# An attention stage: pixels' softmax in pieces of 128, and the norm's squares on ScalarE

## The chip, the core and the metric

The kernel runs as one launch on one core of a Trainium2 chip. The metric is the device time of that launch in microseconds (us), as the median of several runs. Engines are named as in the profile: PE is TensorE's matmul stream, PEld its weight loads, DVE is VectorE, ACT is ScalarE, POOL is GpSimd, SP is SyncE, which issues most transfers.

## The reference

Four layers follow one another on an image tensor x of 32 x 192 x 56 x 56 in float32. Each adds to x a function of its group norm (32 groups of 6 channels): agent attention, a scan over the pixels in both directions, a shift with a small blur, and a long convolution by FFT. The change lies in the first layer alone:

```python
def _gn(v, G=32, eps=1e-5):                 # mean and variance of a group: 6 channels, all pixels
    m = mean(g); s = var(g)
    return (g - m) / sqrt(s + eps)

q, k, v = split(xf @ Wqkv + bqkv)           # n = 3136 pixels, 6 heads of 32 channels
agent = q averaged over 8 x 8 pixels        # 49 agents
agent_attn = softmax(agent * scale @ k.T + pos_bias, over the pixels)
agent_v = agent_attn @ v                    # 49 values for each head
q_attn = softmax(q * scale @ agent.T + agent_bias, over the 49 agents)
out = q_attn @ agent_v + depthwise_3x3(v)
x = x + out @ proj_w + proj_b
```

`pos_bias` and `agent_bias` are sums of a 7 x 7 grid that is enlarged linearly to 56 x 56, a term for each row and a term for each column.

## The kernel before, in words

The attention stage runs from about 147 to 4985 us and goes through the 32 images one after the other. An image lies in SBUF as two tiles: channels 0 to 127 (`x[0]`, 128 x 3136), and channels 128 to 191 with the upper half of the rows on partitions 0 to 63 and the lower half on 64 to 127 (`x[1]`, 128 x 1568). The columns are cut into four chunks of 16, 16, 16 and 8 (`WIDTHS`). A wide chunk holds 896 pixels, the narrow one 448.

The logits of attention need no q and k of their own: `seen` (L582) multiplies the agents into the weights, which gives `gk` and `gq` (128 rows for the first channels) and `gk_c`, `gq_c`. These last hold the other 64 channels and a row of ones, and below them constant coefficients, by which the same matmul adds the bias: 28 rows for the pixel rows of one half of the image, 16 for the columns and 16 for a 4 x 4 part of the grid. There is one set of such coefficients for each chunk and half, eight in all; the first 65 rows are the same in each and are copied to all of them by one DMA for each image (L593, on SP's queue, from the tile `once`).

For one image the code does this.
- For each chunk j: `weigh(j)` (L651) makes the logits of 98 agent rows (two heads) against the pixels on TensorE, takes their maximum on VectorE (`low`, L661) and the exponential on ScalarE (`pr`, L663); `turn_v` and `turn` transpose; `gather` (L697) multiplies by v, `settle` (L711) sorts the heads; `find_v` makes v of a later chunk, `convolve` (L634) makes the depthwise convolution by eight products and sums on VectorE (L646). `moments` (L507) of the next image stands after the last chunk.
- `ask(0)`, then `join` (L721), which makes `values`. `ask(j)` (L743) is the pixels' softmax: pieces of 112 pixels on the partitions, 294 columns (6 heads of 49 agents). Two pieces share a PSUM tile; each takes a matmul over the first channels (L751) and one over the rest with the bias (L752), a maximum (L755) and a subtraction (L756) on VectorE. Four pieces share an exponential on ScalarE (L764), a sum (L766), a reciprocal and a product (L768) on VectorE.
- For t from 1 to 5: `ask(t)`; `turn_back(t-1)` (L771), in which TensorE transposes the pieces (L778) and ScalarE copies the three results to `pqT` (L782); `project(t-2)` (L799), which multiplies by the projection, adds the image and lets ScalarE take squares for the next layer's norm (L819); and `answer(t-1)` (L786), whose matmuls multiply `pqT` by `values` (L791, L796), added on VectorE (L793, L797). Between them lies the next image's preparation: `spread_of` (L545) at t = 1, `scaling` (L555) and `normed` (L596) at t = 2 and after, `find_agents` at t = 2.

The next image's group norm comes from `moments` and two small matmuls. `moments` takes mean and variance of each partition by VectorE's bn_stats over seven pieces of `x[0]` (L512) and four of `x[1]` (L514) and aggregates them (L516, L517). It also sums 8 pixels each (`by_x`, L521) for the agents' average. `grouped` (L538) averages over a group's channels with a constant matrix; `spread_of` uses it for the mean and forms the squared difference from it (`d`), `scaling` uses it for the variance.

The tile framework puts the instructions in order on each engine and inserts the waits. An engine works strictly in its own order. The PSUM pool has four tiles of two banks; the SBUF tag "weights", which `pr` and `pqT` share, has five buffers, "turned" two.

Of the kernel before, what the change touches and what calls it, by code (L numbers as in the profile page):

```python
# [20 lines left out]
F32 = mybir.dt.float32  # L21
# [385 lines left out]
class _Ready:  # L407


    def __init__(self, pool, images):  # L410
        self.images = images

        def new(name, shape):
            return pool.tile(shape, F32, name=name, tag=name)

        self.w, self.c, self.k = new("att_w", [128, 1240]), new("att_c", [65, 770]), new("att_k", [128, 704])
        self.gk_c, self.gq_c = (new(n, [128, 2 * len(WIDTHS), HA]) for n in ("gk_c", "gq_c"))
        self.xs_c = [new(f"xs_c{j}", [128, S * w]) for j, w in enumerate(WIDTHS)]

    def image(self, nc, a, b):  # L420
# [17 lines left out]
def attention(ctx: ExitStack, tc: tile.TileContext, a, ready, x1, st_a, st_c, beside):  # L438
# [16 lines left out]
    UP, LOW = slice(0, 64), slice(64, 128)  # L455
    HALVES = ((0, UP), (1, LOW))
    P2 = slice(0, PAIR)

    def psum():
        return pp.tile([128, 2, BANK], F32, name="ps", tag="ps")  # L460
# [30 lines left out]
    def small(name, shape):  # L491
        return sp.tile(shape, F32, name=name, tag=name)
# [5 lines left out]
    def sizes(j):  # L498
        w = WIDTHS[j]
        return w, 28 * w, 28 * w // SUB  # L500
# [5 lines left out]

    def moments(x):  # L507

        st_a, st_c = small("st_a", [128, 7, 6]), small("st_c", [128, 4, 6])
        flat = [t.rearrange("p y x -> p (y x)") for t in x]  # L510
        for i in range(7):
            nc.vector.bn_stats(st_a[:, i], flat[0][:, i * 448 : (i + 1) * 448])  # L512
        for i in range(4):
            nc.vector.bn_stats(st_c[:, i], flat[1][:, i * 392 : (i + 1) * 392])  # L514
        mv = small("mv", [128, 2, 2])
        nc.vector.bn_aggr(mv[:, 0], st_a.rearrange("p a b -> p (a b)"))  # L516
        nc.vector.bn_aggr(mv[:, 1], st_c.rearrange("p a b -> p (a b)"))  # L517
        pool_a, pool_c = small("pool_a", [128, AG]), small("pool_c", [65, AG])
        by_x = [wp.tile([128, n, POOL], F32, name="by_x", tag=f"by_x{n}", bufs=1) for n in (S, S // 2)]
        for t in range(2):  # L520
            nc.vector.tensor_reduce(  # L521
                by_x[t].rearrange("p y q -> p (y q)"), x[t].rearrange("p y (q x) -> p (y q) x", x=8), AX.X, ALU.add
            )
        nc.vector.tensor_reduce(
            pool_a.rearrange("p (w q) -> p w q", w=POOL), by_x[0].rearrange("p (w y) q -> p w q y", y=8), AX.X, ALU.add
        )
        fours = small("fours", [64, 2 * POOL, POOL])
        for h, r in HALVES:
            nc.vector.tensor_reduce(
                fours[:, h * POOL : (h + 1) * POOL], by_x[1][r].rearrange("p (w y) q -> p w q y", y=4), AX.X, ALU.add  # L530
            )
        nc.vector.tensor_tensor(
            pool_c[0:64].rearrange("p (w q) -> p w q", w=POOL), fours[:, 0::2], fours[:, 1::2], ALU.add
        )
        nc.vector.memset(pool_c[64:65], 1.0)
        return mv, (pool_a, pool_c)
# [5 lines left out]
                mm(ps[:, 0, t : t + 1], norm4[:, 2 * s + t], src[s], start=(s == 0), stop=(s == 1))  # L542
        return ps[:, 0, 0:2]

    def spread_of(mv):  # L545

        mean = small("mean", [128, 2])
        nc.vector.tensor_copy(mean, grouped([mv[:, t, 0:1] for t in range(2)]))
        d = small("d", [128, 2])
        nc.vector.tensor_tensor(d, mv[:, :, 0], mean, ALU.subtract)  # L550
        nc.vector.tensor_tensor(d, d, d, ALU.mult)
        nc.vector.tensor_tensor(d, d, mv[:, :, 1], ALU.add)
        return mean, d

    def scaling(mean, d, pools):  # L555
# [26 lines left out]
    def seen(ag, w, to_c, name):  # L582

        ps = psum()
        for i, cols in enumerate((slice(0, 128), slice(128, C + 1))):
            n = (128, 65)[i]
            mm(ps[:n, i, : 4 * AG], w[0][:, cols], ag[0], start=True, stop=True)
            mm(ps[:n, i, 4 * AG : HA], w[1][:, cols], ag[1], start=True, stop=True)
        g = small(name, [128, HA])
        nc.scalar.copy(g, ps[:, 0, :HA])  # L590
        c = sp.tile([65, HA], F32, name="once", tag="once", bufs=1)
        nc.scalar.copy(c, ps[0:65, 1, :HA])
        nc.sync.dma_start(out=to_c[0:65], in_=c.unsqueeze(1).to_broadcast([65, 2 * NK, HA]))  # L593
        return g

    def normed(x, rs, nb, j):  # L596
# [54 lines left out]
    def weigh(j, g, low, sums):  # L651
        _, n, _ = sizes(j)
        prs = []
        for p in range(3):
# [7 lines left out]
            pr = wp.tile([PAIR, 2, CH], F32, name="pr", tag="weights", bufs=5)  # L662
# [77 lines left out]
        return values  # L740


    def ask(j, g):  # L743
        _, _, ns = sizes(j)
        pq = wp.tile([SUB, 8, HA], F32, name="pq", tag="turned", bufs=2)
        for q0 in range(0, 2 * ns, 4):
            for q in range(q0, q0 + 4, 2):
                ps = psum()
                for i in range(2):
                    px = slice((q + i) * SUB, (q + i + 1) * SUB)  # L750
                    mm(ps[:SUB, i, :HA], xs_a[j][:, px], g, start=True, stop=False)  # L751
                    mm(ps[:SUB, i, :HA], xs_c[j][0:KC, px], gq_c[0:KC, 2 * j + (q + i) // ns], start=False, stop=True)  # L752
                by_head = ps[:SUB, :, :HA].rearrange("p i (h g) -> p i h g", g=AG)
                mx = sp.tile([SUB, 2, HEADS], F32, name="mx", tag="mx", bufs=4)
                nc.vector.tensor_reduce(mx, by_head, AX.X, ALU.max)  # L755
                nc.vector.tensor_tensor(  # L756
                    pq[:, q : q + 2].rearrange("p i (h g) -> p i h g", g=AG),
                    by_head,
                    _bc(mx, [SUB, 2, HEADS, AG]),
                    ALU.subtract,  # L760
                )
            flat = pq[:, q0 : q0 + 4].rearrange("p i c -> p (i c)")
            rows = flat.rearrange("p (r g) -> p r g", g=AG)
            nc.scalar.activation(flat, flat, AF.Exp)  # L764
            sm = sp.tile([SUB, 4 * HEADS], F32, name="sm", tag="sm", bufs=4)
            nc.vector.tensor_reduce(sm, rows, AX.X, ALU.add)  # L766
            nc.vector.reciprocal(sm, sm)
            nc.vector.tensor_tensor(rows, rows, _bc(sm, [SUB, 4 * HEADS, AG]), ALU.mult)  # L768
        return pq

    def turn_back(j, pq):  # L771
        _, n, ns = sizes(j)
        out = []
        for p in range(3):
            ps = psum()
            for q in range(2 * ns):
                h, s = divmod(q, ns)
                nc.tensor.transpose(  # L778
                    ps[P2, h, s * SUB : (s + 1) * SUB], pq[:, q, p * PAIR : (p + 1) * PAIR], ident[:SUB, :SUB]
                )  # L780
            t = wp.tile([PAIR, 2, CH], F32, name="pqT", tag="weights", bufs=5)
            nc.scalar.copy(t[:, :, :n], ps[P2, :, :n])  # L782
            out.append(t)
        return out

    def answer(j, pqT, values, o):  # L786
        _, n, _ = sizes(j)
        ps = psum()
        for h in range(2):
            for p, r in HALVES:  # L790
                mm(ps[r, h, :n], values[:, p], pqT[p][:, h, :n], start=True, stop=True)  # L791
        got = o[0].rearrange("p (h n) -> p h n", h=2)
        nc.vector.tensor_tensor(got, got, ps[:, :, :n], ALU.add)  # L793
        ps = psum()
        for h, r in HALVES:
            mm(ps[r, 0, :n], values[:, 2], pqT[2][:, h, :n], start=True, stop=True)  # L796
        nc.vector.tensor_tensor(o[1], o[1], ps[:, 0, :n], ALU.add)  # L797

    def project(j, o, x, st):  # L799
# [23 lines left out]

    nxt = ready.first
    mv, pools = moments(nxt)
    rs, nb = scaling(*spread_of(mv), pools)
    ag = find_agents(0, pools)
    gk = seen(ag, wkT, gk_c, "gk_a")
    for j in range(NK):
# [3 lines left out]
    for b in range(NB):  # L833
# [1063 lines left out]
    return np.stack([w[0:128], np.pad(w[128:C], ((0, 64), (0, 0)))], 1)  # L1897


def _coefficients(grid, cols, rows):  # L1900

    grid, cols, rows = grid.reshape(HA, POOL, POOL), cols.reshape(HA, S), rows.reshape(HA, S)
    out = np.zeros((KC - 65, 2 * len(WIDTHS), HA), grid.dtype)
    for j, w in enumerate(WIDTHS):
        for h in range(2):
            to = out[:, 2 * j + h]
            to[0:28] = rows[:, 28 * h : 28 * h + 28].T
            to[28 : 28 + w] = cols[:, STARTS[j] : STARTS[j] + w].T
            to[44:60] = grid[:, 3 * h : 3 * h + 4, GRID[j] : GRID[j] + 4].reshape(HA, 16).T
    return out  # L1910


def _laid_out(inputs):
# [22 lines left out]
    out["coef_q"] = _coefficients(a["L0_conv_na_bias"], cols, rows)  # L1936
# [41 lines left out]
```

## Time and profile before

| what | us |
|---|---|
| median of 3 runs | 10783.73 |
| lowest and highest | 10777.28, 10800.41 |
| profiled execution, its own time | 10811.08 |
| its span in the trace | 10809.3 |
| mean granted TensorE clock | 0.95 of full speed |

The page of the profile gives, for the whole span, 9604.3 us of PE (89%), 9260.0 us of DVE (86%), 6372.8 us of ACT (59%) and 2918.0 us of POOL (27%). In the attention stage POOL does nothing. The transfer that ends an image (L888) is issued 32 times, the first at 347.2 us and the last at 4983.8, so an image takes 149.6 us on average.

A row of the timeline gives start and duration in us, the engine, the line, the operation with its output and inputs, partitions x elements and type, the number of instructions put together, and in brackets the idle time before with what ended it. A row of a group gives busy time, mean ns of one, and idle time before with what ended it. A window's row is explained where it is shown.

### The profile page before, as it was taken

How to read it: one execution, taken by the hardware profiler on the slowest of the kernel's cores; microseconds unless marked ns; L12 is line 12 of the kernel's file. 1: busy time of each engine (PE TensorE's matmuls, PEld its weight loads, DVE VectorE, ACT ScalarE, POOL GpSimd, SP SyncE). 2: the span in 40 equal slices, each digit the busy share in tenths (PEclk: the TensorE clock that was granted, in tenths of full speed). 3: DMA queues.
4: the chain of work that ended last, by engine and by line, in shares of the span. 5: the costliest groups of instructions: out<-in, count | busy, mean ns of one | idle time of the engine just before them, and what ended most of it. 6: DMA issues, size and time to landing. Idle time of an engine off the chain costs nothing. (4 is left out here: it accounts for less than half of the span.)

```text
span 10809.3 us, 166766 instructions
## 1 busy us (share of the span) xinstructions
PE 9604.3 (89%) x64806; PEld 5959.0 (55%) x64806; DVE 9260.0 (86%) x11668; ACT 6372.8 (59%) x11964; POOL 2918.0 (27%) x2614
## 2 busy tenths in 40 slices
PE   6999999999999999998888888888888799999998
PEld 3555555555555555554333333333333577787876
DVE  5888888888888888887999999999999577777877
ACT  3555555555555555554666666666666466666766
POOL 0000000000000000002655555555555444444441
PEclk8999999999999999998999999999999899999999
DMA  4211221112121111111344333333444589999998
GB/s 122 63 47 49 63 64 63 37 58 63 64 63 35 61 46 46 46 34 56 92 102 98 97 97 97 97 97 97 97 101 103 153 269 273 274 275 273 278 274 264
DMA packets 1104877, 1240.31 MB, mean 115 GB/s; under 512 B 773091, under 2 KB 807200, under 8 KB 1091992
## 3 DMA queue, kind: packets, MB, share of 16 engines
q1 hardware_dynamic: 1083148, 1201.53, 38.8%
q10 hardware_dynamic: 20932, 28.02, 1.0%
q8 instruction: 516, 8.45, 0.3%
q14 instruction: 281, 2.30, 0.1%
HBM read 915.94 MB, written 306.43 MB: 113 GB/s over the span
## 5 line engine op out<-in xcount | busy, mean ns | idle before, releaser
L646 DVE SCALAR_TENSOR_TENSOR o<-v_a,att_w,o 128x896 f32<-128x896 f32 (+1 forms) x1024 | 1053.3, 1029 | 421.7 <-ACT v_a L620 296.6
L1163 POOL MEMSET f<- 128x1 f32 x96 | 8.8, 98 | 4842.7 <-DMA st_c<-st 4837.7
L1543 DVE STREAM_TRANSPOSE z<-turned 128x1792 f32<-128x1792 f32 x192 | 677.4, 3528 | 258.3 <-ACT turned L1543 257.8
L1543 ACT COPY y<-ps 64x252 f32<-64x252 f32 (+1 forms) x2304 | 784.0, 340 | 157.9 <-PE ps L1543 128.1
L1156 ACT ACTIVATE q<-q 128x784 f32<-128x784 f32 x384 | 328.3, 855 | 813.6 <-DVE q L1151 638.5
L663 ACT ACTIVATE pr<-ps,low 98x896 f32<-98x896 f32 (+1 forms) x384 | 352.3, 918 | 567.8 <-DVE low L661 567.8
L911 PE MATMUL ps<-sq,fixed 128*128 128x392 f32 x512 | 296.8, 742 | 427.7 <-ACT sq L1234 427.7
L764 ACT ACTIVATE pq<-pq 112x1176 f32<-112x1176 f32 x224 | 265.3, 1184 | 683.3 <-DVE pq L756 654.1
L751 PE MATMUL ps<-gq_a,xs_a 128*112 128x294 f32 x1792 | 609.0, 422 | 46.6 <-DVE pq L756 24.1
L1543 POOL TENSOR_TENSOR xn<-x,scale 128x896 f32<-128x896 f32 x192 | 328.4, 1711 | 1192.3 <-DMA x<-x 759.4
L646 DVE SCALAR_TENSOR_TENSOR o<-v_c,att_w,o 128x448 f32<-128x448 f32 (+1 forms) x1024 | 634.3, 619 | 7.5 <-ACT v_c L631 2.4
L659 PE MATMUL ps<-xs_a,gk_a 128*98 128x448 f32 (+1 forms) x1536 | 638.9, 497 | 0.0
L660 PE MATMUL ps<-xs_c,gk_c 125*98 125x448 f32 (+1 forms) x1536 | 631.3, 492 | 0.0
L911 PE MATMUL ps<-x,weights 128*128 128x392 f32 x1536 | 573.7, 516 | 31.1 <-DVE bv L1185 14.1
L752 PE MATMUL ps<-gq_c,xs_c 125*112 125x294 f32 x1792 | 581.4, 411 | 0.0
L1543 PEld LDWEIGHTS ps<-toep,y 128*32 128x32 f32 x16896 | 508.2, 151 | 113.4 <-ACT y L1543 109.2
L1543 PE MATMUL ps<-toep,y 128*32 128x112 f32 x16896 | 554.8, 287 | 0.0
L1543 PE MATMUL ps<-rows,xn 128*112 128x112 f32 x3072 | 378.5, 281 | 159.6 <-POOL xn L1543 136.0
L1543 ACT ACTIVATE turned<-ps,rs 128x448 f32<-128x448 f32 (+1 forms) x576 | 384.4, 668 | 203.4 <-PE ps L1543 195.7
L1543 PE MATMUL ps<-fixed,padded 128*128 128x168 f32 x3072 | 490.0, 314 | 0.0
L766 DVE TENSOR_REDUCE sm<-pq 112x24 f32<-112x1176 f32 x224 | 307.7, 1374 | 181.9 <-ACT pq L764 181.9
L1543 PEld LDWEIGHTS ps<-fixed,padded 128*128 128x128 f32 x3072 | 455.6, 195 | 2.4 <-issue 1.9
(367 smaller groups left out, 25548.6 us busy)
## 6 DMA issues: line engine op xcount, KB each, us to landing
toep<-spans SPq DMA_DIRECT2D x192, 2352.0 KB
x<-x SPq DMA_DIRECT2D x576, 392.0 KB
x<-x SPq DMA_DIRECT2D x896, 196.0 KB
out_x<-done SPq DMA_DIRECT2D x384, 196.0 KB
spans<-lags SPq DMA_DIRECT2D x24, 2352.0 KB
x<-in_x SPq DMA_DIRECT2D x32, 1568.0 KB
x<-x SPq DMA_DIRECT2D x32, 1568.0 KB
x<-in_x SPq DMA_DIRECT2D x64, 392.0 KB
```

The source lines that it names most:

```text
L646: nc.vector.scalar_tensor_tensor(dst, tap(i), dww[:, t, i : i + 1], dst, ALU.mult, ALU.add)
L659: mm(ps[P2, h, :n], g[:, cols], xs_a[j][:, px], start=True, stop=False)
L660: mm(ps[P2, h, :n], gk_c[0:KC, 2 * j + h, cols], xs_c[j][0:KC, px], start=False, stop=True)
L663: nc.scalar.activation(pr[:, :, :n], ps[P2, :, :n], AF.Exp, bias=low[:, j, p : p + 1], accum_out=sums[:, j, p : p + 1])
L751: mm(ps[:SUB, i, :HA], xs_a[j][:, px], g, start=True, stop=False)
L752: mm(ps[:SUB, i, :HA], xs_c[j][0:KC, px], gq_c[0:KC, 2 * j + (q + i) // ns], start=False, stop=True)
L764: nc.scalar.activation(flat, flat, AF.Exp)
L766: nc.vector.tensor_reduce(sm, rows, AX.X, ALU.add)
L911: mm(out, aa, srcs[t][h], start=True, stop=False)
L1156: nc.scalar.activation(den, den, AF.Ln)
L1163: nc.gpsimd.memset(s, 0.0)
L1543: return lambda *args, **kw: self.tc.keep_in_program_order(do(*args, **kw))
```

## The change: pieces of 128 pixels, and squares about the mean

For the three wide chunks, `ask` and `turn_back` use seven pieces of 128 pixels in place of eight of 112. The fourth piece lies across the two halves of the image (the last 64 pixels of one and the first 64 of the other), so it gets a set of coefficients of its own: for each wide chunk a third one, made of 14 rows of either half and of the grid rows that they need. `gq_c` grows from 8 to 11 sets. The pieces are grouped as 2 + 2 and 2 + 1. The narrow chunk keeps four pieces of 112.

The norm's second moment is no longer taken by bn_stats. `moments` sums `by_x` to one number for each partition and tile. `spread_of` makes the group's mean from it, and ScalarE then squares x about that mean in six instructions of 784 elements that sum their results; VectorE adds the parts. The squares write to a tile of the tag "weights", whose buffers are cut from five to four.

```diff
-        self.gk_c, self.gq_c = (new(n, [128, 2 * len(WIDTHS), HA]) for n in ("gk_c", "gq_c"))
+        self.gk_c, self.gq_c = (
+            new(n, [128, k, HA]) for n, k in (("gk_c", 2 * len(WIDTHS)), ("gq_c", 2 * len(WIDTHS) + 3))
+        )
...
+    WB = 4
...
     def moments(x):
-        st_a, st_c = small("st_a", [128, 7, 6]), small("st_c", [128, 4, 6])
-        flat = [t.rearrange("p y x -> p (y x)") for t in x]
-        for i in range(7):
-            nc.vector.bn_stats(st_a[:, i], flat[0][:, i * 448 : (i + 1) * 448])
-        for i in range(4):
-            nc.vector.bn_stats(st_c[:, i], flat[1][:, i * 392 : (i + 1) * 392])
-        mv = small("mv", [128, 2, 2])
-        nc.vector.bn_aggr(mv[:, 0], st_a.rearrange("p a b -> p (a b)"))
-        nc.vector.bn_aggr(mv[:, 1], st_c.rearrange("p a b -> p (a b)"))
...
         for t in range(2):
             nc.vector.tensor_reduce(
                 by_x[t].rearrange("p y q -> p (y q)"), x[t].rearrange("p y (q x) -> p (y q) x", x=8), AX.X, ALU.add
             )
+            nc.vector.tensor_reduce(mv[:, t : t + 1], by_x[t].rearrange("p y q -> p (y q)"), AX.X, ALU.add)
...
-    def spread_of(mv):
-        mean = small("mean", [128, 2])
-        nc.vector.tensor_copy(mean, grouped([mv[:, t, 0:1] for t in range(2)]))
-        d = small("d", [128, 2])
-        nc.vector.tensor_tensor(d, mv[:, :, 0], mean, ALU.subtract)
-        nc.vector.tensor_tensor(d, d, d, ALU.mult)
-        nc.vector.tensor_tensor(d, d, mv[:, :, 1], ALU.add)
+    def spread_of(x, mv):
+        for t in range(2):
+            nc.vector.tensor_scalar(mv[:, t : t + 1], mv[:, t : t + 1], 1.0 / (N // (1 + t)), None, ALU.mult)
+        mean, away = small("mean", [128, 2]), small("away", [128, 2])
+        nc.vector.tensor_copy(mean, grouped([mv[:, t : t + 1] for t in range(2)]))
+        nc.vector.tensor_scalar(away, mean, -1.0, None, ALU.mult)
+        parts, d = small("parts", [128, 6]), small("d", [128, 2])
+        for i in range(6):
+            t, y = (0, 14 * i) if i < 4 else (1, 14 * (i - 4))
+            sq = wp.tile([128, 2 * CH], F32, name="sq", tag="weights", bufs=WB)
+            nc.scalar.activation(
+                sq[:, : 14 * S], x[t][:, y : y + 14].rearrange("p y x -> p (y x)"), AF.Square, bias=away[:, t : t + 1],
+                accum_out=parts[:, i : i + 1],
+            )
+        nc.vector.tensor_reduce(d[:, 0:1], parts[:, 0:4], AX.X, ALU.add)
+        nc.vector.tensor_reduce(d[:, 1:2], parts[:, 4:6], AX.X, ALU.add)
+        for t in range(2):
+            nc.vector.tensor_scalar(d[:, t : t + 1], d[:, t : t + 1], 1.0 / (N // (1 + t)), None, ALU.mult)
         return mean, d
...
-        nc.sync.dma_start(out=to_c[0:65], in_=c.unsqueeze(1).to_broadcast([65, 2 * NK, HA]))
+        nc.sync.dma_start(out=to_c[0:65], in_=c.unsqueeze(1).to_broadcast([65, to_c.shape[1], HA]))
...
+    def pieces(j):
+        if WIDTHS[j] < 16:
+            return SUB, [2 * j + k // 2 for k in range(4)]
+        return 128, [2 * j + k // 4 if k != 3 else 2 * NK + j for k in range(7)]
+
     def ask(j, g):
-        _, _, ns = sizes(j)
-        pq = wp.tile([SUB, 8, HA], F32, name="pq", tag="turned", bufs=2)
-        for q0 in range(0, 2 * ns, 4):
-            for q in range(q0, q0 + 4, 2):
+        m, which = pieces(j)
+        n = len(which)
+        pq = wp.tile([128, n, HA], F32, name="pq", tag="turned", bufs=2)[:m]
+        for q0 in range(0, n, 4):
+            e = min(q0 + 4, n)
+            for q in range(q0, e, 2):
+                u = min(q + 2, e)
                 ps = psum()
-                for i in range(2):
-                    px = slice((q + i) * SUB, (q + i + 1) * SUB)
-                    mm(ps[:SUB, i, :HA], xs_a[j][:, px], g, start=True, stop=False)
-                    mm(ps[:SUB, i, :HA], xs_c[j][0:KC, px], gq_c[0:KC, 2 * j + (q + i) // ns], start=False, stop=True)
+                for k in range(q, u):
+                    px = slice(k * m, (k + 1) * m)
+                    mm(ps[:m, k - q, :HA], xs_a[j][:, px], g, start=True, stop=False)
+                    mm(ps[:m, k - q, :HA], xs_c[j][0:KC, px], gq_c[0:KC, which[k]], start=False, stop=True)
...
     def turn_back(j, pq):
-            for q in range(2 * ns):
-                h, s = divmod(q, ns)
-                nc.tensor.transpose(
-                    ps[P2, h, s * SUB : (s + 1) * SUB], pq[:, q, p * PAIR : (p + 1) * PAIR], ident[:SUB, :SUB]
-                )
-            t = wp.tile([PAIR, 2, CH], F32, name="pqT", tag="weights", bufs=5)
-            nc.scalar.copy(t[:, :, :n], ps[P2, :, :n])
+            ps = psum().rearrange("p a b -> p (a b)")
+            for k in range(n):
+                nc.tensor.transpose(ps[P2, k * m : (k + 1) * m], pq[:, k, p * PAIR : (p + 1) * PAIR], ident[:m, :m])
+            t = wp.tile([PAIR, 2 * CH], F32, name="pqT", tag="weights", bufs=WB)
+            nc.scalar.copy(t[:, : n * m], ps[P2, : n * m])
...
             if more and t == 1:
-                mean, d = spread_of(mv)
+                mean, d = spread_of(nxt, mv)
```

More of the change, by code (lines that the diff above doesn't have):

```diff
@@ L507, in moments @@
     def moments(x):
-        st_a, st_c = small("st_a", [128, 7, 6]), small("st_c", [128, 4, 6])
-        flat = [t.rearrange("p y x -> p (y x)") for t in x]
-        for i in range(7):
-            nc.vector.bn_stats(st_a[:, i], flat[0][:, i * 448 : (i + 1) * 448])
-        for i in range(4):
-            nc.vector.bn_stats(st_c[:, i], flat[1][:, i * 392 : (i + 1) * 392])
-        mv = small("mv", [128, 2, 2])
-        nc.vector.bn_aggr(mv[:, 0], st_a.rearrange("p a b -> p (a b)"))
-        nc.vector.bn_aggr(mv[:, 1], st_c.rearrange("p a b -> p (a b)"))
-        pool_a, pool_c = small("pool_a", [128, AG]), small("pool_c", [65, AG])
+        pool_a, pool_c, mv = small("pool_a", [128, AG]), small("pool_c", [65, AG]), small("mv", [128, 2])
         by_x = [wp.tile([128, n, POOL], F32, name="by_x", tag=f"by_x{n}", bufs=1) for n in (S, S // 2)]
@@ L661, in weigh @@
             nc.vector.tensor_reduce(low[:, j, p : p + 1], ps[P2, :, :n], AX.XY, ALU.max, negate=True)
-            pr = wp.tile([PAIR, 2, CH], F32, name="pr", tag="weights", bufs=5)
+            pr = wp.tile([PAIR, 2, CH], F32, name="pr", tag="weights", bufs=WB)
             nc.scalar.activation(
@@ L740, in join @@
         return values
+    def pieces(j):
+        if WIDTHS[j] < 16:
+            return SUB, [2 * j + k // 2 for k in range(4)]
+        return 128, [2 * j + k // 4 if k != 3 else 2 * NK + j for k in range(7)]
     def ask(j, g):
-        _, _, ns = sizes(j)
-        pq = wp.tile([SUB, 8, HA], F32, name="pq", tag="turned", bufs=2)
-        for q0 in range(0, 2 * ns, 4):
-            for q in range(q0, q0 + 4, 2):
-                ps = psum()
-                for i in range(2):
-                    px = slice((q + i) * SUB, (q + i + 1) * SUB)
[L751 to L754, printed above, removed]
+        m, which = pieces(j)
[5 more added lines that the diff above has]
+                u = min(q + 2, e)
+                ps = psum()
+                for k in range(q, u):
+                    px = slice(k * m, (k + 1) * m)
+                    mm(ps[:m, k - q, :HA], xs_a[j][:, px], g, start=True, stop=False)
+                    mm(ps[:m, k - q, :HA], xs_c[j][0:KC, px], gq_c[0:KC, which[k]], start=False, stop=True)
+                by_head = ps[:m, : u - q, :HA].rearrange("p i (h g) -> p i h g", g=AG)
+                mx = sp.tile([128, 2, HEADS], F32, name="mx", tag="mx", bufs=4)[:m, : u - q]
@@ L755, in ask @@
                 nc.vector.tensor_reduce(mx, by_head, AX.X, ALU.max)
                 nc.vector.tensor_tensor(
-                    pq[:, q : q + 2].rearrange("p i (h g) -> p i h g", g=AG),
+                    pq[:, q:u].rearrange("p i (h g) -> p i h g", g=AG),
                     by_head,
-                    _bc(mx, [SUB, 2, HEADS, AG]),
+                    _bc(mx, [m, u - q, HEADS, AG]),
                     ALU.subtract,
                 )
-            flat = pq[:, q0 : q0 + 4].rearrange("p i c -> p (i c)")
+            flat = pq[:, q0:e].rearrange("p i c -> p (i c)")
@@ L763, in ask @@
             rows = flat.rearrange("p (r g) -> p r g", g=AG)
             nc.scalar.activation(flat, flat, AF.Exp)
-            sm = sp.tile([SUB, 4 * HEADS], F32, name="sm", tag="sm", bufs=4)
+            sm = sp.tile([128, 4 * HEADS], F32, name="sm", tag="sm", bufs=4)[:m, : (e - q0) * HEADS]
             nc.vector.tensor_reduce(sm, rows, AX.X, ALU.add)
             nc.vector.reciprocal(sm, sm)
-            nc.vector.tensor_tensor(rows, rows, _bc(sm, [SUB, 4 * HEADS, AG]), ALU.mult)
+            nc.vector.tensor_tensor(rows, rows, _bc(sm, [m, (e - q0) * HEADS, AG]), ALU.mult)
@@ L769, in ask @@
         return pq
     def turn_back(j, pq):
-        _, n, ns = sizes(j)
+        m, which = pieces(j)
+        n = len(which)
         out = []
         for p in range(3):
-            ps = psum()
-            for q in range(2 * ns):
-                h, s = divmod(q, ns)
-                nc.tensor.transpose(
-                    ps[P2, h, s * SUB : (s + 1) * SUB], pq[:, q, p * PAIR : (p + 1) * PAIR], ident[:SUB, :SUB]
-                )
-            t = wp.tile([PAIR, 2, CH], F32, name="pqT", tag="weights", bufs=5)
-            nc.scalar.copy(t[:, :, :n], ps[P2, :, :n])
+            ps = psum().rearrange("p a b -> p (a b)")
[3 more added lines that the diff above has]
+            nc.scalar.copy(t[:, : n * m], ps[P2, : n * m])
@@ L790, in answer @@
             for p, r in HALVES:
-                mm(ps[r, h, :n], values[:, p], pqT[p][:, h, :n], start=True, stop=True)
+                mm(ps[r, h, :n], values[:, p], pqT[p][:, h * n : (h + 1) * n], start=True, stop=True)
         got = o[0].rearrange("p (h n) -> p h n", h=2)
@@ L795, in answer @@
         for h, r in HALVES:
-            mm(ps[r, 0, :n], values[:, 2], pqT[2][:, h, :n], start=True, stop=True)
+            mm(ps[r, 0, :n], values[:, 2], pqT[2][:, h * n : (h + 1) * n], start=True, stop=True)
         nc.vector.tensor_tensor(o[1], o[1], ps[:, 0, :n], ALU.add)
@@ L825, in attention @@
     mv, pools = moments(nxt)
-    rs, nb = scaling(*spread_of(mv), pools)
+    rs, nb = scaling(*spread_of(nxt, mv), pools)
     ag = find_agents(0, pools)
@@ L1897, in _by_rows, with _coefficients @@
     return np.stack([w[0:128], np.pad(w[128:C], ((0, 64), (0, 0)))], 1)
-def _coefficients(grid, cols, rows):
+def _coefficients(grid, cols, rows, middle=0):
     grid, cols, rows = grid.reshape(HA, POOL, POOL), cols.reshape(HA, S), rows.reshape(HA, S)
-    out = np.zeros((KC - 65, 2 * len(WIDTHS), HA), grid.dtype)
+    out = np.zeros((KC - 65, 2 * len(WIDTHS) + middle, HA), grid.dtype)
     for j, w in enumerate(WIDTHS):
@@ L1909, in _coefficients @@
             to[44:60] = grid[:, 3 * h : 3 * h + 4, GRID[j] : GRID[j] + 4].reshape(HA, 16).T
+    for j in range(middle):
+        to = out[:, 2 * len(WIDTHS) + j]
+        to[:] = out[:, 2 * j]
+        to[0:14] = out[0:14, 2 * j + 1]
+        to[44:60] = grid[:, [3, 4, 2, 3], GRID[j] : GRID[j] + 4].reshape(HA, 16).T
     return out
@@ L1935, in _laid_out @@
     rows, cols = (np.swapaxes(a[f"L0_conv_{n}_bias"].reshape(HEADS, S, AG), 1, 2) for n in ("ha", "wa"))
-    out["coef_q"] = _coefficients(a["L0_conv_na_bias"], cols, rows)
+    out["coef_q"] = _coefficients(a["L0_conv_na_bias"], cols, rows, 3)
     out["scan_w"] = np.concatenate(
```

## The prediction

> **What bounds the kernel now.** I read the page first, then a table of windows, then TensorE's waits in the attention stage (350 to 4980 us), then the timeline of one image, engine by engine.
>
> The windows (stretch, its length, then busy time and instructions of PE, PEld, DVE, ACT, POOL, then granted clock, DMA share, GB/s) show a stage that is TensorE's: 191 of 200 us, VectorE next, ScalarE with 86 us free.
> ```profile
> 2400.00:2600.00 200.00, 191.00 (x1038) 114.97 (x1038) 161.60 (x246) 113.66 (x199) 0.00 (x0) 0.97 0.15 46
> ```
> TensorE's waits there (total us, times, longest) say where the other 9 us go. The first, 3.1 us once per image, is the largest:
> ```profile
> PE ps L542 <- DVE pq L756: 70.9, 23, 3.1
> PE ps L911 <- DVE o L793: 31.7, 30, 1.1
> PE ps L778 <- ACT pqT L782: 26.0, 33, 1.0
> PE ps L751 <- DVE pq L756: 24.1, 30, 0.9
> ```
> The timeline of TensorE at that place (start, duration, line; the idle time before in brackets):
> ```profile
> 2542.04 0.66 PE L752 MATMUL ps<-gq_c,xs_c 125*112 125x294 f32 x2
> 2545.78 1.84 PE L542 MATMUL ps<-mv,att_k 128*128 128x1 f32 x8 [3.08 <-DVE pq L756]
> 2547.81 4.31 PE L778 MATMUL ps<-att_k,pq 112*98 112x112 f32 x24 [0.19 <-DVE pq L756]
> 2552.05 1.72 PE L791 MATMUL ps<-pqT,values 98*64 98x448 f32 x8
> 2553.61 0.92 PE L796 MATMUL ps<-pqT,values 98*64 98x448 f32 x4
> 2554.46 0.75 PE L751 MATMUL ps<-gq_a,xs_a 128*112 128x294 f32 x2
> 2562.50 0.95 PE L542 MATMUL ps<-d,att_k 128*128 128x1 f32 x8
> 2567.23 1.77 PE L911 MATMUL ps<-o,att_w 128*128 128x448 f32 x4 [0.23 <-ACT pqT L782]
> ```
> VectorE is the late one there: it works without a break from 2476.5 to about 2552.6, and ask(1)'s last subtraction ends at 2551.0. On ScalarE the three copies of turn_back(0) end at 2553.1, and answer(0) and ask(2) follow:
> ```profile
> 2550.27 0.76 DVE L756 TENSOR_TENSOR pq<-ps,mx 112x588 f32<-112x588 f32 x1
> 2551.16 0.10 DVE L548 COPY mean<-ps 128x2 f32<-128x2 f32 x1
> 2551.28 1.38 DVE L768 TENSOR_TENSOR pq<-pq,sm 112x1176 f32<-112x1176 f32 x1
> 2552.16 0.91 ACT L782 COPY pqT<-ps 98x896 f32<-98x896 f32 x1 [0.21 <-PE ps L778]
> ```
> From ask(2) on to the next image TensorE hardly stops. So what delays ask(2) is paid.
>
> **The clock.** The stall has a second price. Around it the granted clock falls to a half:
> ```profile
> 2541.36:2544.77 3.41, 1.34 (x6) 0.64 (x4) 3.41 (x5) 0.00 (x0) 0.00 (x0) 1.00 0.02 5
> 2544.77:2548.18 3.41, 2.21 (x10) 2.18 (x11) 3.41 (x6) 0.42 (x1) 0.00 (x0) 0.50 0.00 0
> 2548.18:2551.60 3.42, 3.42 (x21) 3.42 (x20) 3.40 (x7) 2.23 (x3) 0.00 (x0) 0.50 0.00 0
> 2551.60:2555.01 3.41, 3.41 (x19) 1.52 (x18) 1.89 (x2) 2.34 (x3) 0.00 (x0) 1.00 0.00 0
> ```
> A stretch of 3.41 us in which TensorE works 1.3 us is followed by half clock, and full clock comes back after a full stretch. The eight tiny L542 matmuls take 1.84 us there and 0.95 us at 2562.50; the 24 transposes 4.31 us. The path doesn't pay for most of this today, because VectorE is late anyway.
>
> **Part 1: pieces of 128 pixels.** A wide chunk's softmax takes 7 pieces instead of 8, so three chunks save 6 matmuls per image. L751 and L752 start 0.248 us apart per record, two records each: 0.497 us per matmul, 6 x 0.497 = 3.0 us of TensorE. The transposes L778 move the same columns: nothing. VectorE saves an eighth of 0.76, 0.76, 1.37 and 1.37 us rows: about 1.3 us per wide chunk. ScalarE's second exponential shrinks from 1176 to 882 elements, 0.3 us. The third set of coefficients makes the copy of `once` into gq_c 11 blocks instead of 8, 0.82 MB instead of 0.60, on SP's queue; it is issued in weigh(0) and first used by ask(0), some 55 us later: nothing. Without that cover it would be, at the stage's 46 GB/s, 5 us an image at most.
>
> **Part 2: the norm's sums.** VectorE loses 7 statistics at 0.53 us, 4 at 0.47 and 0.4 of aggregates: 6.0 us; it gains small reduces, scales and one negation, about 1 us. ScalarE gets six squares of 784 elements. The nearest rows are its squares in project, which start 1.03 us apart at 896 elements and 0.65 at 448, accumulator read included; so 0.94 each, 5.6 us. Bounds: 0.65 and 1.03 each, 3.9 to 6.2 us; I take 0.94, between them by size.
>
> By the Trainium skill's page ScalarE: Activation LUTs ("What ACT_TABLE_LOAD costs" has the times of an ACTIVATE) such an instruction with one pointer operand takes 280 ns + 0.833 ns per element, less 93 ns back to back; as an estimate 0.84 us each, 5.0 us for six, without an accumulator read. By it the forecast would be 0.6 us an image lower, some 19 us in all; the rows of project, which have the read, stand nearer.
>
> If all that were hidden, an image would lose 3.0 us of TensorE work and the 3.1 us stall.
>
> **Part 3: where the squares stand.** This decides. spread_of is still called at t = 1, after ask(1) and before turn_back(0). In the changed kernel's order ScalarE has: both exponentials of ask(1), six squares, the three copies pqT of turn_back(0), ask(2)'s exponential. Before, nothing of the norm was on ScalarE there. The squares need `away`, which VectorE makes from the group's mean; in its order this is behind ask(1)'s first product and second sum. So:
> - Ask(0) and ask(1) start and run quicker. The statistics no longer stand between the convolution and ask(0), but TensorE's first pair, ready at 2527.5 today, comes about 1.4 later (the gather's wait of part 4), 2528.9, where today mx starts at 2530.12; so VectorE's relief of 5 us is worth only 1.2 us; the shorter rows give 1.5. The last subtraction ends about 2548.3 instead of 2551.0.
> - Behind it come reciprocal and mean 0.3, product 1.38, sum 1.03 (three quarters of 1.37), away 0.1: 2551.2.
> - Six squares: 2556.9. Three copies, 0.81 us start to start: 2559.5, against 2553.1. Answer(0), whose matmuls wait for them, and ask(2), queued behind it on TensorE: about 2561.0 against 2554.46, **+6.5 us**.
> - Ask(2) has two matmuls less, -1.0; the 1.0 us stall before the later L778 rows and the 0.23 at L911 go, since what they wait for is long done. At project: **+4.2 us**.
> - VectorE's sums of the squares stand ahead of its addition L793 and of ask(2)'s maxima, but both wait for PE work that comes later anyway: nothing. The buffers of "weights" go from 5 to 4; each reuse waits for work that TensorE does earlier in its order: nothing, and 0.3 us if a square waits for the one before.
>
> **Part 4: the clock after it.** TensorE now idles some 10 us in that place, in two pieces around the transposes. It resumes at half clock, which lasts for the rest of the stretch it resumes in and, unless that rest is nearly whole, for one more: 3.4 to 5.1 us on average, I take 4.6, in which half the work is lost, +2.3. In the middle of convolve(2), the 3.35 us reduction by_x now stands where three statistics (1.67 us) stood, ahead of the maxima `low` that the exponentials, the turned weights and the gather of chunk 1 wait for; the gather then waits 2.1 us instead of 0.59, which may bring one more slow window: +0.8. The short slow stretch after the 1.0 us stall, in every other image, goes: -0.85. Together +2.2. Bounds of the clock's part: -0.85 (the lost slow stretch alone) and +5 (slow until two full windows). I take 2.2, as the rows above show a return after one.
>
> The Trainium skill's page TensorE: Matmul & The Clock Gate ("What's actually happening") has the clock fall after an idle window and return after a busy one. The row with 1.3 us of work in its window disagrees, since that window wasn't idle. By the page the gather's 2.1 us would cost no clock, and the sum would be 0.8 us an image, 25 us in all, lower. Its advice against gaps of over 3 us ("Why this matters for your kernels") speaks against this change.
>
> **The sum.** 4.2 + 2.2 = 6.4 us an image; 31 images have a next one: +198. The first image's norm has nothing beside it: by_x (5.1 us) and the squares (5.6) now both come before its first normed pixel, where the statistics were done at 78 us, before the matmuls that wait for other loads (147): +11 at most, which I take. The last image has neither squares nor statistics, -3. Together +206 on the profiled execution of 10811 us: 11,017. The median of the runs was 27 us lower: **10,990 us**.
>
> **The rivals.**
> - Slower without the clock: resumption at full speed, 31 x 4.2 + 8 = +138, 10,922 from the median. For: the half clock today is mostly hidden. Against: TensorE has work only for half of the windows before ask(2).
> - Slower, with more: two slow windows each image, 4.2 + 4.6 = 9 us an image, 31 x 9 + 8 = +287, 11,071.
> - **Faster**: the squares run before turn_back(0) is ready. It decides where `away` is there 6 us ahead of the first transpose's end, thus about 2543. Then each image loses 3.0 + 3.1 us: -190, 10,594; half of it, 10,690, if they fit in part. For: VectorE is relieved by 5 us before ask(0) and ScalarE is free from 2538.7 to 2547.8. Against: the order puts `away` behind ask(1)'s exponentials.
> - No change: the whole of VectorE's 7 us is had before ask(1)'s end (2544), which cancels the +6.5: within 20 us of 10,784. It fails where TensorE paces ask(0), as 2528.9 says.
>
> **How the numbers follow.** Forecast 0.50; without the clock 0.20; more clock 0.15; faster 0.11; no change 0.04. About 0.2% (22 us) is what a measurement can tell. Faster 0.11, same 0.04, slower 0.85. The range, 10,820 to 11,110, leaves out the faster cases and the top of the strongest clock.
>
> **What would show it.** L542's first matmul earlier than before, ScalarE with six squares back to back right before the three pqT copies, TensorE waiting there some 10 us for pqT, ask(2) starting 6 us later in its image, and periods of about 156 us instead of 150. Wrong, if the copies come first, or the squares lie inside ask(1), or VectorE's end of ask(1) moves by more than 5 us.

## The result: 1.7% slower

The changed kernel takes 10968.62 us (median of 4 runs, 10958.75 to 10980.63) against 10781.09 us (median of 4, 10777.28 to 10800.41): a ratio of 1.0171, 95% interval 1.0156 to 1.0186. Between the medians lie 187.5 us. The profiled execution took 10972.2 us, its span is 10970.4 us. In the traces the attention stage is the place: the transfer that ends the last image is issued at 5158.8 us instead of 4983.8, 175 us later. The stages behind it, whose code is unchanged, differ by 14 us the other way in these two executions. Over the traces of all the kernels here they take 5801 to 5842 us, counted from the stage's last matmul on `pqT`, so 14 us there says nothing about the change.

The page's first part shows what the change saved. Against the figures of before, 42 us of PE and 237 us of DVE are gone and ACT has 141 us more. Every engine's sum but ScalarE's fell, and the time rose:
```profile
PE 9562.4 (87%) x64134; PEld 5948.1 (54%) x64134; DVE 9023.1 (82%) x11444; ACT 6513.9 (59%) x12348; POOL 2910.8 (27%) x2614
```
TensorE's waits in the attention stage of the changed kernel (350 to 5170 us; total us, times, longest) have a new head, answer(0) waiting for the copies pqT, in 30 images and up to 7.5 us in each. The wait for ask(1)'s subtractions, first before, is longer too:
```profile
PE ps L804 <- ACT pqT L795: 203.9, 30, 7.5
PE ps L537 <- DVE pq L771: 119.1, 30, 4.2
PE ps L684 <- ACT pr L669: 37.3, 30, 1.2
PE ps L924 <- DVE o L806: 33.2, 32, 1.1
```
The same place of an image on TensorE, to set against the timeline of before. The transposes of turn_back(0) end at 2484.4; answer(0) comes 6.77 us later. Its first seven records take 3.30 us, where eight took 1.72 before (a matmul of this kind leaves two records, a transpose one). ask(2) starts at 2495.66:
```profile
2473.08 0.66 PE L767 MATMUL ps<-gq_c,xs_c 125*128 125x294 f32 x2
2477.95 1.84 PE L537 MATMUL ps<-mv,att_k 128*128 128x1 f32 x8 [4.22 <-DVE pq L771]
2479.65 4.70 PE L793 MATMUL ps<-att_k,pq 128*98 128x128 f32 x21
2491.12 3.30 PE L804 MATMUL ps<-pqT,values 98*64 98x448 f32 x7 [6.77 <-ACT pqT L795]
2495.66 0.76 PE L766 MATMUL ps<-gq_a,xs_a 128*128 128x294 f32 x2
```
VectorE and ScalarE in the same stretch say why. `mean` is there at 2482.1, but `away` stands behind the product (L783) and the sum (L781) of ask(1); the squares follow at once, 0.93 us start to start (four of them are left out here), and the three copies, whose data were ready at 2484.4, come after the sixth:
```profile
2481.41 0.46 DVE L771 TENSOR_TENSOR pq<-ps,mx 128x294 f32<-128x294 f32 x1
...
2481.99 0.10 DVE L545 COPY mean<-ps 128x2 f32<-128x2 f32 x1
2482.11 1.38 DVE L783 TENSOR_TENSOR pq<-pq,sm 128x1176 f32<-128x1176 f32 x1
2483.41 1.06 DVE L781 TENSOR_REDUCE sm<-pq 128x18 f32<-128x882 f32 x1
2484.39 0.16 DVE L546 TENSOR_SCALAR away<-mean 128x2 f32<-128x2 f32 x1
```
```profile
2481.90 0.94 ACT L779 ACTIVATE pq<-pq 128x882 f32<-128x882 f32 x1 [2.14 <-DVE pq L771]
2484.58 0.95 ACT L551 ACTIVATE sq<-x,away 128x784 f32<-128x784 f32 x1 [1.74 <-DVE away L546]
...
2489.26 0.93 ACT L551 ACTIVATE sq<-x,away 128x784 f32<-128x784 f32 x1
2490.09 0.19 ACT L551 ACTIVATION_READ_ACCUMULATOR sq<-x,away 128x1 f32 x1
2490.19 2.48 ACT L795 COPY pqT<-ps 98x896 f32<-98x896 f32 x3
```
The windows of the same stretch (columns as in the prediction) show the clock. Each of the two stretches without TensorE work is followed by half clock (0.50); the second slow one, 2487.84 to 2494.66, holds answer(0):
```profile
2474.18:2477.59 3.41, 0.00 (x0) 0.00 (x0) 3.41 (x6) 0.00 (x0) 0.00 (x0) 1.00 0.00 0
2477.59:2484.42 6.83, 6.39 (x29) 5.80 (x29) 6.81 (x12) 2.12 (x2) 0.00 (x0) 0.50 0.00 0
2484.42:2487.84 3.42, 0.00 (x0) 0.00 (x0) 1.43 (x4) 3.26 (x7) 0.00 (x0) 1.00 0.00 0
2487.84:2494.66 6.82, 3.54 (x9) 1.42 (x11) 0.62 (x4) 4.83 (x9) 0.00 (x0) 0.50 0.00 0
```

### The profile page after: what moved, and what is told of

Its sections match the earlier page's. It is cut to its first block, busy times and chain, and to the rows that moved or that the text cites. A ratio compares the mean times of both kernels' runs of the same rounds, so it can differ in the third digit from the quotient of the medians.

```text
span 10970.4 us, 165798 instructions
## 1 busy us (share of the span) xinstructions
PE 9562.4 (87%) x64134; PEld 5948.1 (54%) x64134; DVE 9023.1 (82%) x11444; ACT 6513.9 (59%) x12348; POOL 2910.8 (27%) x2614
## 5 line engine op out<-in xcount | busy, mean ns | idle before, releaser
L779 ACT ACTIVATE pq<-pq 128x1176 f32<-128x1176 f32 (+2 forms) x224 | 241.9, 1080 | 888.7 <-DVE pq L771 888.6
L766 PE MATMUL ps<-gq_a,xs_a 128*128 128x294 f32 (+1 forms) x1600 | 544.3, 426 | 0.0
L767 PE MATMUL ps<-gq_c,xs_c 125*128 125x294 f32 (+1 forms) x1600 | 526.1, 417 | 0.0
L770 DVE TENSOR_REDUCE mx<-ps 128x12 f32<-128x588 f32 (+1 forms) x448 | 307.2, 700 | 260.9 <-PE ps L767 260.9
## 6 DMA issues: line engine op xcount, KB each, us to landing
gq_c<-once SPq DMA_DIRECT2D x32, 821.1 KB
```

Of the source, the lines that this page charges most:

```text
L766: mm(ps[:m, k - q, :HA], xs_a[j][:, px], g, start=True, stop=False)
L767: mm(ps[:m, k - q, :HA], xs_c[j][0:KC, px], gq_c[0:KC, which[k]], start=False, stop=True)
```

## Where an image's time goes, stretch by stretch

The image is cut at five first starts on TensorE: weigh(0), weigh(3), ask(0), answer(0), ask(2), answer(1). Means over the third to the 23rd image of each profiled execution, in us. The names of the experiments are explained below.

| kernel | weigh(0) to weigh(3) | to ask(0) | to answer(0) | to ask(2) | to answer(1) | to the next image | period |
|---|---|---|---|---|---|---|---|
| before | 52.54 | 9.28 | 30.27 | 2.64 | 17.79 | 38.56 | 151.07 |
| changed | 53.41 | 9.28 | 33.23 | 5.27 | 16.00 | 39.02 | 156.20 |
| pieces alone | 52.54 | 9.27 | 28.43 | 2.79 | 15.05 | 38.98 | 147.06 |
| squares alone | 53.40 | 9.28 | 35.59 | 5.31 | 17.20 | 38.98 | 159.77 |
| squares later | 53.40 | 9.28 | 25.73 | 2.61 | 15.08 | 39.00 | 145.09 |
| squares earlier | 53.40 | 12.04 | 25.13 | 2.58 | 14.92 | 38.63 | 146.70 |
| earlier, sums on ScalarE | 53.41 | 12.04 | 23.42 | 2.57 | 14.92 | 38.64 | 145.00 |
| half squares | 53.41 | 9.28 | 31.27 | 5.30 | 15.33 | 39.01 | 153.60 |
| six unread matmuls | 53.40 | 9.28 | 33.23 | 4.47 | 15.53 | 39.01 | 154.92 |
| eight unread matmuls | 53.40 | 9.28 | 33.23 | 3.60 | 15.08 | 39.01 | 153.60 |

Against before, the changed kernel loses 0.87 us ahead of weigh(3), 2.96 up to answer(0) and 2.63 in answer(0); it gets back 1.79 from ask(2) to answer(1), and loses 0.46 later: +5.13. The last of these stands alike in the runs with the pieces alone and with the squares alone, 0.42 each; it isn't traced.

## The experiments

The theory (A in the expectations): the loss is the place of the squares in ScalarE's order, ahead of the copies pqT, and the half clock after it; the pieces of 128 and the relief of VectorE are gains. The rivals: the pieces with their coefficients and the lost buffer cost time; squares on ScalarE cost the same anywhere; the clock is hidden.

**Each half of the change alone (e1, e2).** e1 keeps the pieces and takes `moments` and `spread_of` from before (here and for e2 only a line of each is shown, with a remark that isn't in the code):
```diff
-    def spread_of(x, mv):          # and moments: sums of by_x, squares on ScalarE
+    def spread_of(mv):             # and moments: bn_stats, as before
```


> The change with the norm's sums as before (bn_stats on VectorE), so pieces of 128 pixels, 11 sets of coefficients and four buffers alone. Theory A (the place of the squares on ScalarE is the whole loss, the pieces are a gain): VectorE's last subtraction of ask(1) comes about 2.1 us earlier in each image (shorter second groups), ask(2) is 1.0 us shorter, the 1.0 us stall at L778 may go: -3 to -4 us in each of 32 images, 10,650 to 10,720 us. Rival B (the pieces, the larger copy of coefficients or the lost buffer cost time by themselves): 10,780 us or more.

Measured: 10719.16 us, ratio 0.9935 (0.9919 to 0.9952) to before. This is the weak end of the expectation. VectorE's last subtraction of ask(1) comes 2.1 us earlier, as expected, and the images of the table are 4.0 us faster than before. The last seven periods are slower than before (149.4 us against 147.6), so the whole gains less. Rival B falls: the pieces are a gain.

e2 keeps the squares and takes `ask`, `turn_back`, `answer` and the eight sets from before:
```diff
-        m, which = pieces(j)       # seven pieces of 128
+        _, _, ns = sizes(j)        # eight pieces of 112, as before
```


> The change with pieces of 112 as before, so the squares on ScalarE, by_x before the maxima and four buffers alone. Theory A: the delay of the squares without what the pieces give back, about +9 us in each image: 11,000 to 11,100 us. Rival B: no change against before, 10,780 us, or at most +2 us in each image.

Measured: 11131.59 us, ratio 1.0313 (1.0296 to 1.033), above the range that was expected, by 32 us. The images of the table lose 8.7 us, about the 9 that were expected; the last seven periods lose 11.6. The squares alone lose nearly twice what the whole change loses. In its trace the same wait leads (total us, times, longest):
```profile
PE ps L795 <- ACT pqT L786: 232.8, 30, 7.9
```

**The lost buffer (e7).** It is the kernel before, with four buffers.
```diff
-            pr = wp.tile([PAIR, 2, CH], F32, name="pr", tag="weights", bufs=5)
+            pr = wp.tile([PAIR, 2, CH], F32, name="pr", tag="weights", bufs=4)
...
-            t = wp.tile([PAIR, 2, CH], F32, name="pqT", tag="weights", bufs=5)
+            t = wp.tile([PAIR, 2, CH], F32, name="pqT", tag="weights", bufs=4)
```


> The kernel before with four buffers of the tag weights instead of five, nothing else. Theory A: nothing, 10,770 to 10,800 us. Rival (the lost buffer is part of the loss): +1 us in each image or more, 10,815 us and above.

Measured: 10800.24 us, ratio 1.0003 (0.9994 to 1.0013). This is the upper end of the expectation, and far from the rival's 10,815. The buffer costs nothing in the kernel before; four against five with the squares in it was not run.

**The squares elsewhere (e3, e4).** `spread_of` is split into `mean_of`, `squares` and `spread`, the work unchanged. e3 calls the squares behind answer(0):
```diff
             if more and t == 1:
-                mean, d = spread_of(nxt, mv)
+                mean, away = mean_of(mv)
             if more and t == 2:
+                d = spread(parts)
...
                 answer(t - 1, back[t - 1], values, done[t - 1])
+            if more and t == 1:
+                parts = squares(nxt, away)
```


> All of the change, but the squares are called after answer(0), so that ScalarE makes the three pqT copies of turn_back(0) first; the sums of the parts are called at t = 2. Theory A: ask(2) starts about 8 us earlier in its image than in the changed kernel and the half clock shrinks: 10,620 to 10,760 us, below the kernel before. Rival C (six squares cost ScalarE, or the norm's chain, the same wherever they stand): 10,900 us or more.

Measured: 10723.49 us, ratio 0.9939 (0.9923 to 0.9956). The six squares are all there, equally long, on the same engine; only their place is another. In ScalarE's timeline the copies now come first, and the squares run under ask(2):
```profile
2340.76 0.91 ACT L804 COPY pqT<-ps 98x896 f32<-98x896 f32 x1 [1.63 <-PE ps L802]
2342.26 0.91 ACT L804 COPY pqT<-ps 98x896 f32<-98x896 f32 x1 [0.59 <-PE ps L802]
...
2345.22 0.95 ACT L555 ACTIVATE sq<-x,away 128x784 f32<-128x784 f32 x1 [0.42 <-DVE away L546]
```
So rival C falls too. In the table ask(2) starts 10.2 us earlier in its image than in the changed kernel, where about 8 were expected. This version takes 145.1 us an image in the table but 152.0 in the last seven periods, where the order on the engines is another and TensorE waits for the norm's sums (`d`) up to 5.7 us.

e4 calls mean and squares before ask(0), with `spread` at t = 2:
```diff
+        if more:
+            mean, away = mean_of(mv)
+            parts = squares(nxt, away)
         asked[0] = ask(0, gq)
```


> All of the change, but mean and squares are called before ask(0), where ScalarE is free; VectorE's sums of the parts then stand before ask(0)'s first maximum and hold it by some 2.8 us. Theory A: pqT isn't late, TensorE has no norm matmul before turn_back(0); 10,620 to 10,740 us, less the 2.8 us where VectorE paces ask(1): up to 10,800. Rival C: 10,900 us or more.

Measured: 10704.67 us, ratio 0.992 (0.9904 to 0.9937). As expected VectorE stands still before ask(0)'s first maximum, because its two sums of the parts come first in its order:
```profile
2337.69 0.16 DVE L564 TENSOR_REDUCE d<-parts 128x1 f32<-128x4 f32 x1 [3.25 <-ACT sq L555]
...
2339.55 0.15 DVE L565 TENSOR_REDUCE d<-parts 128x1 f32<-128x2 f32 x1 [1.52 <-ACT sq L555]
...
2339.81 0.76 DVE L779 TENSOR_REDUCE mx<-ps 128x12 f32<-128x588 f32 x1
```

**Without VectorE's wait (e6).** Two small ScalarE instructions with an accumulator take the place of the sums and scales, and stand right behind the squares, before ask(0):
```diff
-        nc.vector.tensor_reduce(d[:, 0:1], parts[:, 0:4], AX.X, ALU.add)
-        nc.vector.tensor_reduce(d[:, 1:2], parts[:, 4:6], AX.X, ALU.add)
-        for t in range(2):
-            nc.vector.tensor_scalar(d[:, t : t + 1], d[:, t : t + 1], 1.0 / (N // (1 + t)), None, ALU.mult)
+        for t, cols in ((0, slice(0, 4)), (1, slice(4, 6))):
+            out = small(f"out{t}", [128, 4])
+            nc.scalar.activation(
+                out[:, : cols.stop - cols.start], parts[:, cols], AF.Identity, scale=1.0 / (N // (1 + t)),
+                accum_out=d[:, t : t + 1],
+            )
```


> The run with early squares, with the two sums of their parts by ScalarE (accumulated in one instruction for each tile), so that VectorE waits for no square before ask(0). Theory A (what is left is VectorE's end of ask(1)): VectorE comes about 2.5 us earlier, 10,620 to 10,690 us. Rival: VectorE's wait was hidden, 10,700 us as with its sums.

Measured: 10672.87 us, ratio 0.9884 (0.9864 to 0.9903), the fastest version that was run. The stretch to answer(0) falls by another 1.7 us. It keeps both ideas of the change and all its squares, and its interval lies below that of the pieces alone: with the squares in a free place, moving the norm's sums off VectorE is a gain after all.

**How long the squares are (e8).** Each square goes over 392 elements, so half of the pixels are left out of the second moment.
```diff
-                sq[:, : 14 * S], x[t][:, y : y + 14].rearrange("p y x -> p (y x)"), ...
+                sq[:, : 7 * S], x[t][:, y : y + 7].rearrange("p y x -> p (y x)"), ...
```


> The changed kernel with each square over 392 elements instead of 784, so half of the pixels are left out of the second moment. Theory A (the path goes through the six squares): by the squares' 0.93 us and some 0.6 us at 392 elements, six times 0.33 us less, 2.0 us in each of 31 images: 10,900 to 10,915 us. Rival (what counts is that pqT's copies wait for away, not the squares' length): 10,960 to 10,980 us.

Measured: 10902.96 us, ratio 1.0104 (1.0084 to 1.0124). The squares of the changed kernel and of this one (shortest, median and longest in ns):
```profile
L551 ACT ACTIVATE sq<-x,away x192: 931/932/948, 172.1 to 4969.2; 128x784 f32<-128x784 f32 x192
L551 ACT ACTIVATE sq<-x,away x192: 604/606/623, 173.3 to 4897.4; 128x392 f32<-128x392 f32 x192
```
A square takes 0.606 us instead of 0.932 (medians), six times the difference is 1.96 us, and the stretch to answer(0) is 1.96 us shorter. The squares lie on the path in their full length.

**The clock (e5, e9).** TensorE gets matmuls that nobody reads while it waits for pqT. Nothing else moves, and the stretch to answer(0) stays at 33.23 us.
```diff
+    def fill(k):
+        ps = psum()
+        for i in range(k):
+            mm(ps[:, 0, :CH], ready.w[:, 0:128], xs_a[0][:, 0:CH], start=True, stop=True)
...
                 back[t - 1] = turn_back(t - 1, asked[t - 1])
+            if more and t == 1:
+                fill(6)
```


> The changed kernel with six more matmuls of 448 columns per image on TensorE, between turn_back(0) and answer(0), whose result nobody reads; they fill most of the 6.8 us in which TensorE waits for pqT. ScalarE and VectorE do as before. Theory A (the slow clock after the wait is on the path): answer(0) runs at full clock, its stretch up to ask(2) falls from 4.5 to about 2.4 us: -1.5 to -2.1 us in each of 31 images, 10,900 to 10,930 us. Rival D (the clock is hidden, the wait is all): no change, 10,960 to 10,980 us, or slower.

Measured: 10923.49 us, ratio 1.0129 (1.0108 to 1.0151), 45 us below the changed kernel's median and inside the expectation. But answer(0) up to ask(2) was only partly faster (4.47 us in the mean, 3.2 to 5.5): some 2 us of the wait were left idle. Hence a second one, with `fill(8)`:

> The changed kernel with eight unread matmuls in the wait for pqT instead of six, since six left 2.0 us of it idle and answer(0) in many images at half clock. Theory A: answer(0) now at full clock in most images (2.4 to 3 us from its start to ask(2), against 5.3 in the changed kernel and 4.4 with six): 10,870 to 10,910 us. Rival D: no better than with six, 10,920 us or more.

Measured: 10894.51 us, ratio 1.0093 (1.0076 to 1.011). The work is more and the time less. From answer(0) to ask(2) it is 3.60 us in the mean, short of the 2.4 to 3 that were expected: 3.2 us in most images, 4.9 in five. On TensorE the gap is nearly closed, and in this image the granted clock is 1.00 over answer(0):
```profile
2439.65 4.69 PE L799 MATMUL ps<-att_k,pq 128*98 128x128 f32 x21
2444.14 6.26 PE L579 MATMUL ps<-xs_a,att_w 128*128 128x448 f32 x16
2451.12 1.40 PE L810 MATMUL ps<-pqT,values 98*64 98x448 f32 x4 [0.72 <-ACT pqT L801]
```
From ask(0) to the next image the two kernels differ only behind the start of answer(0): 1.67 us in it and 0.92 behind it, 2.6 us an image. Rival D falls; the half clock after the wait was on the path. The slow stretch behind the other wait, the 4.2 us for ask(1)'s subtractions, stays in these runs; what it costs was not measured.

## Why the prediction came out right, point by point

- **Where the squares stand.** As forecast: `away` came 2.7 us behind the last subtraction (2.9 forecast), the six squares took 5.6 us up to the copies (5.6 forecast), the copies 2.5. The experiments with the squares elsewhere show that this place is the loss: e3 and e4 take it away with the same work.
- **VectorE's end of ask(1)** was mis-sized. Counted from the start of weigh(3), the first maximum was expected 2.6 us earlier and came 3.0 earlier (17.4 to 14.4 us); the last subtraction was expected 4.1 us earlier and came 5.1 earlier (38.3 to 33.3). The prediction called itself wrong if this end moved by more than 5 us. Its own times, 2551.0 to 2548.3, count from weigh(0): so counted 2.7 us were forecast and 4.2 came, inside that limit; counted from weigh(3) the move lies just above it. From weigh(3) to ask(2) the sum has 6.5 less the 1.5 ahead of weigh(3), and 2.3 for the clock: 7.3 us. Measured are 2.96 + 2.63 = 5.6. This is the largest miss: 1.0 us of it is VectorE's end, 0.3 us are `away` and the copies, and 0.4 us isn't traced.
- **The clock behind it** was put at +2.3. Against before, answer(0) up to ask(2) grew by 2.63 us. The filled kernels show the clock's share: eight unread matmuls give back 1.67 us there and 0.92 behind ask(2), 2.6 in all, and at least that, since in some images answer(0) still ran slow.
- **The gather's wait** was put at 2.1 us instead of 0.59, and +0.8 for a slow window. Its place is now the transposes of v (L684), 1.24 us, for the same reason (`pr` waits for `low` behind by_x; its row stands in the result, the gather's of before below this item). The stretch grew by 0.87 us, and the clock stayed at 1.00 around each of these waits in the trace. This term was 1.4 us too large in all. On it the Trainium skill's page TensorE: Matmul & The Clock Gate ("What's actually happening") was nearer: no idle window, no loss of clock. Where a window with 1.3 us of work was followed by half clock in the kernel before, the measurement still decides against its rule.
```profile
PE ps L706 <- ACT pr L663: 18.2, 31, 0.6
```
- **ask(2) to answer(1)**: -2.2 for two matmuls and two stalls, and -0.85 for the clock were forecast, -1.79 came. With eight unread matmuls it is -2.71: so 0.92 us of the slow clock behind the wait for `pqT` falls into this stretch, and the prediction had nothing of it there. Of the 1.00 us stall, 0.29 is left.
- **The sum**: 6.4 us an image forecast, 5.1 in the middle of the stage and 5.9 in the last seven periods, where the kernel before was faster (147.6 against 151.1 us) and nothing was forecast apart. The errors partly cancel: 1.7 us too much up to ask(2) and 1.4 for the gather's wait, against 1.3 us that didn't come back behind ask(2) and 0.46 later that had no term.
- **Ahead of the loop** +11 was forecast, and the first `values` come 12.9 us later (290.9 us against 278.1). That this fits is partly luck. The first normed pixels come 28 us later (180.6 us against 152.5), but the first weigh(0) only 6.3 (198.4 against 192.1); the rest is mainly one wait for `pr` in the first image, 10.6 us where it was 2.3 before. The last image gave 4.1 us back, where 3 were forecast.
- **The signs.** As forecast: the group mean's matmuls come earlier, six squares stand back to back right before the three copies, ask(2) starts 6.5 us later in its image (6 forecast), and the period is 156.2 us (156). The wait for `pqT` is 6.8 us, not some 10: the 10 were both waits around the transposes, which measure 4.2 and 6.8.
- **Parts at nothing.** The buffer is shown for the kernel before (e7). The coefficients' larger copy (821.1 KB instead of 597.2) isn't isolated, but e1 includes it and gains 4 us an image in the table. VectorE's sums of the squares are done at 2490.7, and its next work waits for TensorE until 2495.0. The pieces' gain per image on TensorE (3.0 us, six matmuls of 0.50) and per chunk on VectorE (1.2 us for the 1.3 forecast) stands in the changed kernel's rows.
- **The rivals.** Faster needed `away` some 6 us earlier. e4 and e6 made this, and got the sign: 0.9884 where 10,594 of 10,784 would be 0.982. What stays there is the wait for ask(1)'s subtractions, 4.2 us in e6, which the rival had let go.

## What to carry to other kernels

Work moved to an engine with idle time is only free if it doesn't stand in that engine's order ahead of something that the bound engine waits for next; read the order at that place, not the busy share. Here ScalarE was 59% busy, and in one place the squares made the kernel 2.4% slower than bn_stats with the same pieces (1.0171 against 0.9935), in another 0.5% faster (0.9884). Price a longer gap on TensorE at its length and at the slow clock behind it.

## What the runs showed that was not expected

The prediction had no thought of matmuls that nobody reads. They made the changed kernel faster, by 74 us with eight in each image, since they kept the granted clock up: in the attention stage half clock lasted 505 us in the changed kernel, 280 with six, 198 with eight, and 242 in the kernel before (sums of the trace's clock records from 350 us up to the last `values`). And a wait of 1.24 us, in a window of 3.41, cost no clock in any of the 30 images that have it.
